# A chunked delta-rule attention on one core: the second chunk served by key and query products with the first chunk's keys in place of a state, and norm products of 96 columns

## The chip, the core and the metric

The kernel runs on one core of one Trainium2 chip, as one launch. The metric is the device time of that core in microseconds (us). The core has five engines with a queue each: TensorE (PE in the profile, with its weight loads as PEld), VectorE (DVE), ScalarE (ACT), GpSimd (POOL) and SyncE (SP), which issues the DMAs. All data are float32.

## What is computed

An input x of 4 sequences x 256 tokens x 256 channels goes through two layers. Each layer has a mixing part and an expert part, and each of the four parts sees its input scaled by a conditioning signal (a decaying two-way scan over the side input). The change lies in the mixing part of the first layer, a gated delta rule with 16 key heads and 32 value heads of 128 dimensions. The reference's scan over chunks, cut to its core:

```python
q = l2norm(q); k = l2norm(k)                  # norms over the 128 dimensions
A = where(strict, -(k_beta @ k.T) * decay, 0)  # within a chunk
attn = solve_triangular(eye - A, eye)
v_c, k_cumdecay = attn @ v_beta, attn @ (k_beta * exp(g))
def step(state, inp):
    attn_i = where(lower, q_i @ k_i.T * d_i, 0)
    v_new = v_i - kcd_i @ state
    o_i = q_i * exp(g_i) @ state + attn_i @ v_new
    state = state * exp(g_last) + (k_i * exp(g_last - g_i)).T @ v_new
    return state, o_i
```

The kernel uses chunks of 128 tokens, so a sequence has two: the first starts from a state of zero, and the only state that is ever read is the one after the first chunk. For the second chunk it holds that k_2 @ state and q_2 @ state are products of k_2 (or q_2) with k_1.T diag(decay) v_new_1.

## The kernel before, in words

The work is done in two halves, s = 0 and 1, of two sequences (b) each: 512 tokens. Attention is cut into units, one for each key head and half, so 32 units with two value heads (v) each; a tile of "four problems" holds v and b, 4 x 128 columns of 128 partitions. Four units make a Group, which does their 32x32 inverses together in one long chain of small VectorE operations (`small_inverses`). Then the units go two by two.

A unit (class Unit) goes through these functions:

- `products`: loads the key and query weights, makes the causal convolution of q and k (ps_cvq, ps_cvk, then ScalarE and three VectorE taps), and keeps both with their channels on partitions, one buffer kq for each chunk n (0 and 1), in which j is 0 for keys and 1 for queries. For each chunk, `gram` multiplies the keys with keys and queries of the same chunk (two products of 256 columns into ps_gram) and the copy `taken` puts them into kqm. `turn` transposes the first chunk's keys (two transposes) and sums the squares of keys and queries, a product with one column of ones for each of the 8 sums, all into ps_kt; a copy puts the transposed keys into k_tok. Then come the norms (k2, ki, kn, eo), the weights c and dc on POOL, and for each chunk the decay tile attnT, fetched by a broadcast DMA, exponentiated and multiplied with kqm on POOL. The products with keys go into the group's X, those with queries stay in attnT.
- `values`: v's convolution (ps_cvv), transposed into vo (ps_vt).
- `inverse` and `Group.inverse64`: 32x32 and 64x64 products (ps_lu, ps_lx, ps_lxu) that make X the full inverse.
- `outputs`: on POOL, kd is k_tok times the decay weight dc (`decayed`). TensorE makes the first new values vn0 = X vo (ps_vn), the state from kd and vn0 (ps_st, copied by ScalarE to state), the first chunk's output (ps_at), and the second chunk's keys with the state (ps_ks), which VectorE takes off the second chunk's values (`without`). Then vn1, and in `second` the second chunk's output from the queries (qe, which POOL multiplies with exp(g) in `queries`) with the state and from attnT with vn1. The gate product z (ps_z) is made here too.
- `normed`: squares summed on ScalarE, a root on POOL, four POOL products on vo, two transposes (ps_ot); `Group.project` multiplies with the output weights (ps_wo) and adds to x.

After attention class Rest does, for each half, 64 small experts, two to a product (ps_h, ps_a), a mixing layer (ps_in, ps_mix, ps_out) and 8 larger experts (ps_e, ps_ae), with routers (ps_lg, ps_w_wT).

The order of instructions on each engine is not the program's order. Every operation is recorded on a Tape with its engine, an estimated cost, the buffers that it reads and writes, a table of activation functions where it needs one, and for TensorE a density (`dense`, 0.12 for `turn`). `Tape.plan` lays all of them out by list scheduling with those costs, each engine taking the most urgent operation among those that could start first, with limits on how many buffers of a kind may be out at once (`MOST`, and PLACES for all tiles of 512 columns) and a penalty for thin TensorE work. Ten rounds are planned, the shortest plan is kept, and the instructions are issued in its order. Everything recorded there has line 128 in the profile, so the groups are told apart by the names of their tiles.

Of the kernel before, what the change touches and what calls it, by code (L numbers as in the profile page):

```python
# [181 lines left out]
class Tape:  # L182
# [11 lines left out]
    def op(self, engine, cost, emit, r=(), w=(), port=False, table=None, due=None, late=0.0, to=None, dense=1.0):  # L194
# [22 lines left out]
        if to is not None and to not in o.bufs:  # L217
            o.bufs.append(to)
            to.uses += 1
# [64 lines left out]
    def plan(self, latest):  # L284
# [17 lines left out]
        while todo:  # L302
# [4 lines left out]
            for e, ops in waiting.items():  # L307
# [10 lines left out]
                if best is not None and first >= best[0]:  # L318
                    continue
# [13 lines left out]
                if best is None or most[2] < best[0]:  # L333
                    best = (most[2], self.ops[most[1]])
# [5 lines left out]
            at, o = best  # L340
# [70 lines left out]
ROUNDS, SWITCH, LOAD, SPARE, AHEAD, EACH, END, IDLE, MOMENT, GAP, RATE, GIVES = 10, 14.0, 1.3, 90.0, 160.0, 15.0, 1300.0, 30.0, 0.8, 150.0, 4.0, 5.0  # L411
UNIT = 33.0
WINDOW, ENOUGH, LITTLE, SLOW, THIN = 3.4, 0.45, 0.38, 0.5, 10.0
# [261 lines left out]
class Unit:  # L675
# [83 lines left out]
    def products(self):  # L759
        p, s, h = self.p, self.s, self.h  # L760
        e, op = p.e, p.tape.op
        ident = p.const(IDENT)
# [14 lines left out]

        kqm = []
# [4 lines left out]
        for n in range(2):  # L783
            ps = p.ps(f"gram{n}_{self.tag}")
            m = self.buf([P, 2, 2, P], "kqm", 2, name=n)
            kqm.append(m)

            def gram(n=n, ps=ps):
                for b in range(2):
                    e.tensor.matmul(  # L790
                        ps()[:, b * 256 : b * 256 + 256],
                        kq[n]()[:, b, 0, :],
                        kq[n]()[:, b].rearrange("p j d -> p (j d)"),
                        start=True,
                        stop=True,
                    )

            op("PE", _mm(256, 2), gram, [kq[n]], [ps], to=m)

            def taken(m=m, ps=ps):  # L800
                copy(
                    m().rearrange("p j b d -> p b j d"),
                    ps().rearrange("p (b j d) -> p b j d", b=2, j=2),
                )

            op(*cost(512), taken, [ps], [m])

        self.k_tok = self.buf([P, 2, P], "k_tok", 5)
        ps = p.ps(f"kt_{self.tag}")
        sums = lambda j: ps()[:, 256 + 4 * j : 260 + 4 * j]  # L810
# [13 lines left out]
        def turn(ps=ps):  # L824
            for b in range(2):
                e.tensor.transpose(ps()[:, b * P : b * P + P], kq[0]()[:, b, 0, :], ident)
            for n in range(2):
                for j in range(2):
                    for b in range(2):
                        at = 2 * n + b  # L830
                        e.tensor.matmul(
                            sums(j)[:, at : at + 1],
                            sqs[n]()[:, b, j, :],
                            p.const(LT)[:, P - 1 :],
                            start=True,
                            stop=True,
                        )

        op("PE", 1.86, turn, [(kq[0], {0}), *sqs], [ps], to=self.k_tok, dense=0.12)
        op(  # L840
            *cost(256),
            lambda ps=ps: copy(
                self.k_tok(), ps()[:, :256].rearrange("p (b d) -> p b d", b=2)
            ),
            [ps],
            [self.k_tok],
        )
# [244 lines left out]
    def outputs(self):  # L1092
        p, s = self.p, self.s
        e, op = p.e, p.tape.op
        vo, kq, gate = self.vo, self.kq[1], p.gateb[s]
# [6 lines left out]
        def vob(n):  # L1102
            return vo[n]().rearrange("p v b d -> p (v b) d")
# [24 lines left out]
        kd = self.buf([P, 2, 2, P], "kd", 1)  # L1128

        def decayed():  # L1130
            w = self.dc().rearrange("p (v b) -> p v b", v=2).unsqueeze(3)
            e.gpsimd.tensor_tensor(
                kd(), _over(self.k_tok(), 1, 2), w.to_broadcast([P, 2, 2, P]), ALU.mult
            )

        op("POOL", 1.05, decayed, [self.k_tok, self.dc], [kd])
        vn0 = new_values(0, lambda: vob(0), vo[0])
        state = four("state", 1)
        ps = product(
            "st", lambda q: kd()[:, q // 2, q % 2, :], lambda q: vn0()[:, q, :], [kd, vn0], state  # L1140
        )
        copied(state, ps, state)
# [9 lines left out]
            lambda q: kq()[:, q % 2, 0, :],  # L1152
            lambda q: state()[:, q, :],
            [(kq, {0}), state],
# [31 lines left out]
        def queries():  # L1186
            to = qe().rearrange("p (v b) d -> p v b d", v=2)
            e.gpsimd.tensor_tensor(to, to, _over(kq()[:, :, 1, :], 1, 2), ALU.mult)

        op("POOL", 1.28, queries, [(kq, {1})], [qe])  # L1190
# [30 lines left out]
        def second():  # L1221
            for q in range(4):
                o = ps()[:, q * P : q * P + P]
                e.tensor.matmul(o, qe()[:, q, :], state()[:, q, :], start=True, stop=False)
                e.tensor.matmul(o, self.attnT[1]()[:, q, :], vn1()[:, q, :], start=False, stop=True)

        op("PE", 2 * cost, second, [qe, state, self.attnT[1], vn1], [ps])
# [80 lines left out]
class Program:  # L1308
# [85 lines left out]
    MOST = {"attnT": 20, "kq1": 10, "kq0": 4, "kqm": 8, "vo": 8, "zs": 6, "oT": 6, "w0": 6, "hw0": 8, "w1": 6, "hw1": 8}  # L1394
# [771 lines left out]
```

## Time and profile before

| what | value |
| --- | --- |
| median of 3 runs | 1534.3 us (1534.11, 1534.3, 1545.77) |
| the profiled execution's own time | 1536.94 us |
| its span in the profile | 1535.0 us |
| mean granted clock of TensorE | 0.957 |
| PE / DVE / ACT / POOL busy | 1431.9 / 1129.4 / 932.5 / 909.9 us |
| instructions | 24434 |
| ACT table loads | 106 at line 128, 136.0 us |

The span runs from the first to the last instruction of the profiled execution; 1.94 us of its time lie around it. An engine's busy time counts its instructions alone. The clock is the share of TensorE's full speed that was granted. A row of the groups gives the tile written and those read, the shape, the count, the busy time in us and the mean length of one in ns, then the idle time of the engine just before them and who ended it. Rows of TensorE show two records for each float32 product and one for a transpose, and their lengths overlap, so that the distance of two starts tells more than a length.

### The profile page before, as it was taken

The page shows a single profiled execution, that of the slowest core. Times are in us where ns is not written, and L with a number is a line of the kernel's source. Part 1 is how long each engine was busy: PE and PEld are TensorE (multiplying, and loading weights), DVE is VectorE, ACT ScalarE, POOL GpSimd, SP SyncE. Part 2 cuts the span into 40 slices and gives each one's busy share as a digit, 9 for nine tenths or more (in the row PEclk, how much of TensorE's full clock was granted, in tenths as well). Part 3 has the DMA queues.
Part 4 walks back from the last instruction along what each step waited for, and adds up shares of the span by engine and source line. Part 5 has one row for each costly group of instructions (what it writes and reads, how often), then busy time and mean ns, then how long its engine had stood idle before and what let it go on. Part 6 is the DMA issues. An engine that isn't in the chain of part 4 may idle for free.

```text
span 1535.0 us, 24434 instructions
## 1 busy us (share of the span) xinstructions
PE 1431.9 (93%) x8620; PEld 933.4 (61%) x8620; DVE 1129.4 (74%) x2117; ACT 932.5 (61%) x2037; POOL 909.9 (59%) x913
## 2 busy tenths in 40 slices
PE   4985999999999799999999999899999999999988
PEld 2643776876877577687777777686443443444433
DVE  7899889579578888988899868875777686343233
ACT  2685887888668788888888887886112441112120
POOL 3159778477483878869777568545766437133032
PEclk9987899999899999989999999899999999999999
DMA  6030212112030320312311222201564434691030
GB/s 211 9 118 7 67 59 83 43 54 64 12 114 15 98 83 25 100 58 68 94 46 57 82 76 84 79 13 36 147 171 137 130 107 130 168 276 50 0 110 14
DMA packets 79801, 126.52 MB, mean 82 GB/s; under 512 B 10032, under 2 KB 26160, under 8 KB 79680
## 3 DMA queue, kind: packets, MB, share of 16 engines
q1 hardware_dynamic: 78672, 123.81, 26.7%
q8 instruction: 68, 1.11, 0.3%
q10 hardware_dynamic: 1008, 1.16, 0.3%
q14 instruction: 53, 0.43, 0.1%
HBM read 120.31 MB, written 4.62 MB: 81 GB/s over the span
## 4 chain that ended last, share of the span: by engine, by line
PE 68%; DVE 17%; POOL 6%; ACT 5%; issue 2%; DMA 2%; SPq 1%; ACTq 0%; DVEq 0%; POOLq 0%
PE ps_wo L128 7%; PE ps_h L128 6%; PE ps_a L128 6%; PE ps_z L128 5%; PE ps_at L128 5%; PE ps_cvv L128 4%; PE ps_e L128 3%; PE ps_ae L128 3%; PE ps_vn L128 3%; PE ps_kt L128 3%; PE ps_cvq L128 2%; PE ps_gram L128 2%; POOL vo L128 2%; PE ps_cvk L128 2%; PE ps_in L128 2%
## 5 line engine op out<-in xcount | busy, mean ns | idle before, releaser
L128 DVE SCALAR_TENSOR_TENSOR accv_v<-ps_cvv,sb_convw,accv_v 128x510 f32<-128x510 f32 (+2 forms) x192 | 141.8, 741 | 16.8 <-ACT accv_v L128 11.7
L128 POOL TENSOR_TENSOR hw_h<-hw_h,r_h 128x512 f32<-128x512 f32 x64 | 84.2, 1318 | 111.8 <-DVE hw_h L128 110.4
L128 ACT ACTIVATE r_h<-ps_h 128x512 f32<-128x512 f32 x64 | 38.2, 597 | 183.7 <-PE ps_h L128 181.5
L128 ACT ACT_TABLE_LOAD x106 | 136.0, 1283 | 7.5 <-DVE sb_xT L128 3.6
L128 PE MATMUL ps_cvv<-ratio,wv 128*128 128x512 f32 x256 | 124.2, 614 | 2.3 <-issue 1.4
L128 PE MATMUL ps_z<-wz,ratio 128*128 128x256 f32 x512 | 119.6, 381 | 3.2 <-DVE accv_v L128 2.8
L128 PE MATMUL ps_h<-ratio,w_w 128*128 128x512 f32 x256 | 117.8, 600 | 3.1 <-DMA w_w<-in_w 3.0
L128 PE MATMUL ps_wo<-oT,wo 128*128 128x512 f32 x256 | 116.4, 608 | 0.0
L128 PE MATMUL ps_a<-hw_h,w_w 128*128 128x512 f32 x256 | 115.3, 593 | 0.7 <-POOL hw_h L128 0.7
L128 PEld LDWEIGHTS ps_z<-wz,ratio 128*128 128x128 f32 x512 | 94.7, 190 | 20.2 <-issue 4.5
L128 POOL TENSOR_TENSOR hw_e<-hw_e,r_e 128x512 f32<-128x512 f32 x32 | 40.5, 1279 | 86.8 <-DVE hw_e L128 86.8
L128 PEld LDWEIGHTS ps_h<-ratio,w_w 128*128 128x128 f32 x256 | 48.4, 192 | 64.3 <-issue 61.2
L128 PE MATMUL ps_gram<-kq 128*128 128x256 f32 x256 | 71.7, 420 | 16.9 <-ACT kqm L128 6.6
L128 DVE TENSOR_TENSOR xs<-xs,prod 128x30 f32<-128x30 f32 (+14 forms) x240 | 81.1, 338 | 8.2
L128 PEld LDWEIGHTS ps_a<-hw_h,w_w 128*128 128x128 f32 x256 | 48.5, 190 | 62.6 <-issue 56.2
L128 PE MATMUL ps_at<-vn,attnT 128*128 128x128 f32 x512 | 85.9, 282 | 0.1
L128 DVE SCALAR_TENSOR_TENSOR hw_h<-ps_h,wb_wb 128x512 f32<-128x512 f32 x64 | 43.7, 687 | 56.9 <-ACT r_h L128 50.8
L128 DVE TENSOR_TENSOR prod<-xs,Rt 128x30 f32<-128x30 f32 (+14 forms) x240 | 78.6, 328 | 9.1 <-ACT xs L128 2.8
L128 POOL TENSOR_TENSOR X<-attnT,kqm 128x512 f32<-128x512 f32 x64 | 84.1, 1333 | 1.9 <-PE ps_vn L128 1.6
L128 PEld LDWEIGHTS ps_wo<-oT,wo 128*128 128x128 f32 x256 | 49.5, 196 | 57.9 <-issue 52.8
L128 ACT ACTIVATE junko<-vo 128x128 f32<-128x128 f32 x256 | 79.3, 310 | 7.2
L128 POOL TENSOR_TENSOR vo<-vo,zs 128x512 f32<-128x512 f32 x64 | 82.3, 1306 | 0.0
(258 smaller groups left out, 3802.0 us busy)
## 6 DMA issues: line engine op xcount, KB each, us to landing
attnT<-G SPq DMA_DIRECT2D x64, 256.0 KB, 4.8
w_w<-in_w SPq DMA_DIRECT2D x64, 256.0 KB, 4.6
wb_wb<-w_rows SPq DMA_DIRECT2D x128, 128.0 KB, 4.1
wqk<-in_wqk SPq DMA_DIRECT2D x32, 256.0 KB, 3.5
wv<-in_wv SPq DMA_DIRECT2D x32, 256.0 KB, 3.0
wz<-in_wz SPq DMA_DIRECT2D x32, 256.0 KB, 2.8
wo<-in_wo SPq DMA_DIRECT2D x32, 256.0 KB, 3.1
qe<-G SPq DMA_DIRECT2D x32, 256.0 KB, 3.4
```

Source lines behind the costliest of these rows:

```text
L128: return self._tc.keep_in_program_order(f(*a, **k))
```

## The change

The state is not formed any more. In `products` a third gram is made for each unit, of the first chunk's keys with the second chunk's keys and queries (`cross`, copied like kqm, by VectorE for the first four units and by ScalarE for the rest); it shares an operation with the second chunk's own gram. The transposes of the first chunk's keys and the copy to k_tok go. In `outputs` the decay weight multiplies the first new values (vd, on POOL, which now reads vn0) in place of the keys, ps_ks is cross times vd, and qe takes the queries' part of cross in place of the queries, so that the second chunk's output is qe with vd. The product ps_st and its copy go.

The 8 sums of squares are now products with 96 columns of a triangle of ones, of which the last one is the sum; they are made from the last to the first, so that each leaves its sum in the column that later ones do not reach. The planner is told a density of 0.7 and a cost of 1.0 for them, where `turn` had 0.12 and 1.86.

The planner changes too: in its non-strict step it takes the engine whose best candidate is the most urgent instead of the one that starts first, an operation can hold several result buffers, and most of its constants and buffer limits have new values. With that the order of instructions is another one on every engine from the start on. Counted in the built programs, TensorE has 64 more products of 256 columns, 256 of 96 columns for 256 of one, 128 products of 128 columns and 64 transposes fewer; ScalarE has 32 copies of state and 28 of k_tok fewer, 28 of cross more, and 100 table loads where there were 108; VectorE has 4 copies of cross for 4 of k_tok; POOL has 32 vd for 32 kd; the DMAs are the same in number.

```diff
-ROUNDS, SWITCH, LOAD, SPARE, AHEAD, EACH, END, IDLE, MOMENT, GAP, RATE, GIVES = 10, 14.0, 1.3, 90.0, 160.0, 15.0, 1300.0, 30.0, 0.8, 150.0, 4.0, 5.0
-UNIT = 33.0
-WINDOW, ENOUGH, LITTLE, SLOW, THIN = 3.4, 0.45, 0.38, 0.5, 10.0
+ROUNDS, SWITCH, LOAD, SPARE, AHEAD, EACH, END, IDLE, MOMENT, GAP, RATE, GIVES = 10, 11.7, 1.3, 106.8, 160.0, 23.99, 1300.0, 30.0, 0.68, 150.0, 3.14, 5.0
+UNIT = 41.74
+WIDE = 96
+WINDOW, ENOUGH, LITTLE, SLOW, THIN = 3.4, 0.54, 0.38, 0.5, 10.0
...
-                if best is not None and first >= best[0]:
+                if self.strict and best is not None and first >= best[0]:
...
-                if best is None or most[2] < best[0]:
-                    best = (most[2], self.ops[most[1]])
+                first = most[2] if self.strict else latest[most[1]]
+                if best is None or first < best[0]:
+                    best = (first, most[2], self.ops[most[1]])
...
+        for pairs in (((0, 0),), ((1, 1), (0, 1))):
...
+                m = self.buf([P, 2, 2, P], "kqm" if n0 == n else "cross", 2, name=n0)
...
-            for b in range(2):
-                e.tensor.transpose(ps()[:, b * P : b * P + P], kq[0]()[:, b, 0, :], ident)
...
-                            sums(j)[:, at : at + 1],
-                            sqs[n]()[:, b, j, :],
-                            p.const(LT)[:, P - 1 :],
...
-        op("PE", 1.86, turn, [(kq[0], {0}), *sqs], [ps], to=self.k_tok, dense=0.12)
...
+            for at in reversed(range(8)):
+                j, n, b = at // 4, at // 2 % 2, at % 2
+                e.tensor.matmul(
+                    ps()[:, 505 + at - WIDE : 505 + at],
+                    sqs[n]()[:, b, j, :],
+                    p.const(LT)[:, P - WIDE :],
...
+        op("PE", 1.0, norms, sqs, [ps], dense=0.7)
...
-        op("POOL", 1.05, decayed, [self.k_tok, self.dc], [kd])
-        vn0 = new_values(0, lambda: vob(0), vo[0])
-        state = four("state", 1)
-        ps = product(
-            "st", lambda q: kd()[:, q // 2, q % 2, :], lambda q: vn0()[:, q, :], [kd, vn0], state
-        )
-        copied(state, ps, state)
+            e.gpsimd.tensor_tensor(vd(), vn0(), _over(self.dc(), 2, P), ALU.mult)
+        op("POOL", 1.06, decayed, [vn0, self.dc], [vd])
...
-            lambda q: kq()[:, q % 2, 0, :],
-            lambda q: state()[:, q, :],
+            lambda q: cross()[:, 0, q % 2, :],
+            lambda q: vd()[:, q, :],
...
-        op("POOL", 1.28, queries, [(kq, {1})], [qe])
+        op("POOL", 1.28, queries, [cross], [qe])
...
-                e.tensor.matmul(o, qe()[:, q, :], state()[:, q, :], start=True, stop=False)
+                e.tensor.matmul(o, qe()[:, q, :], vd()[:, q, :], start=True, stop=False)
...
-    MOST = {"attnT": 20, "kq1": 10, "kq0": 4, "kqm": 8, "vo": 8, "zs": 6, "oT": 6, "w0": 6, "hw0": 8, "w1": 6, "hw1": 8}
+    MOST = {'attnT': 20, 'kq1': 12, 'kq0': 2, 'kqm': 8, 'cross': 10, 'vo': 8, 'zs': 6, 'oT': 6, 'w0': 6, 'hw0': 8, 'w1': 6, 'hw1': 8, 'wo': 2, 'sq': 4, 'r0': 3, 'wqk': 20}
```

## The prediction

> **What bounds the kernel now.** I read the page's busy shares first, then the chain that ended last, then the windows by stage, then TensorE's groups and its timeline. From the page, PE's busy share and granted clock in 40 slices, and the chain by engine:
>
> ```profile
> PE 1431.9 (93%) x8620; PEld 933.4 (61%) x8620; DVE 1129.4 (74%) x2117; ACT 932.5 (61%) x2037; POOL 909.9 (59%) x913
> PEclk9987899999899999989999999899999999999999
> PE 68%; DVE 17%; POOL 6%; ACT 5%; issue 2%; DMA 2%; SPq 1%; ACTq 0%; DVEq 0%; POOLq 0%
> ```
>
> The windows by stage: from the first gates to the first new values, to 402, to the end of attention, the experts. After the length stand PE, PEld, DVE, ACT, POOL busy (with counts), PE's granted clock, DMA share and GB/s:
>
> ```profile
> 36.80:167.30 130.50, 103.25 (x593) 66.04 (x593) 115.02 (x233) 89.70 (x173) 76.53 (x78) 0.84 0.15 48
> 167.30:402.00 234.70, 230.68 (x1873) 174.91 (x1873) 188.07 (x359) 199.69 (x461) 166.82 (x168) 0.99 0.19 56
> 402.00:1068.00 666.00, 646.16 (x5077) 488.10 (x5076) 551.21 (x1071) 526.91 (x1212) 457.13 (x464) 0.96 0.21 65
> 1068.00:1535.00 467.00, 437.46 (x1035) 194.71 (x1033) 247.34 (x412) 105.43 (x177) 195.78 (x186) 0.97 0.41 119
> ```
>
> From 167 us on TensorE is busy 96% of the time and no other engine over 85%: a microsecond of TensorE work, or of its clock, is a microsecond of time. Only from 36.8 to 167 is VectorE the bound (115 of 130.5 us busy); there TensorE work is nearly free. The clock has places of its own; in windows of PE alone, the third number is its busy time, the one after the count its clock:
>
> ```profile
> 402.00:420.00 18.00, 17.89 (x185) 0.62 0.02 4
> 552.00:558.00 6.00, 6.00 (x71) 0.72 0.11 37
> 666.00:684.00 18.00, 18.00 (x268) 0.72 0.24 75
> 792.00:804.00 12.00, 12.00 (x156) 0.72 0.30 86
> ```
>
> PE is busy in these and yet granted 0.62 to 0.72. In each the timeline shows a run of thin products just before: 32x32 and 64x64 tiles of the inverses, and in the last three a ps_kt, whose products have one column. The loss is 18 x 0.38 + 6 x 0.28 + 18 x 0.28 + 12 x 0.28 = 16.9 us.
>
> Prices, from the timeline at full clock (start, length, operation; the step to the next start is the price):
>
> ```profile
> 258.54 0.44 PE L128 MATMUL ps_kt<-sb_consts,kq 128*128 128x128 f32 x2 [0.34 <-ACT oT L128]
> 258.82 1.84 PE L128 MATMUL ps_kt<-sb_consts,sq 128*128 128x1 f32 x16
> 260.52 7.11 PE L128 MATMUL ps_wo<-oT,wo 128*128 128x512 f32 x16
> 267.47 3.62 PE L128 MATMUL ps_gram<-kq 128*128 128x256 f32 x16
> 271.02 0.69 PE L128 MATMUL ps_lu<-Tc,X 32*32 32x32 f32 x32
> 273.47 1.04 PE L128 MATMUL ps_vt<-sb_consts,accv_v 128*128 128x128 f32 x8
> 274.35 1.89 PE L128 MATMUL ps_z<-wz,ratio 128*128 128x256 f32 x8
> ```
>
> A matmul has two records. 16 one-column records step 1.70 us (0.106 each); 8 of 128 columns 0.88 (0.110 each); 16 of 256 columns, which are four gram operations, 3.55 (0.89 each; 0.865 at 221.33, which I take).
>
> **The change, part by part.** 32 units run it.
>
> *TensorE work.* Gone per unit: two transposes of k_tok (0.21 at 175.83) and the four products st (8 records, 0.90 at 230.97). Added: the cross gram, 0.865. 32 x (0.865 - 1.11) = -7.8 us. The norms keep 16 records; with 96 columns a record lies between 0.106 and 0.110, so 0 to +0.07 a unit, 0 to +2 us; I take 0, since 96 columns are less than the 128 that already hide.
> By the Trainium skill's page "TensorE: Matmul & The Clock Gate", section "Back-to-back issue gap", a product costs N / 2.4 + 2.5 ns with a floor of 25 ns; one column would then cost 25 and 96 columns 42.5 ns, which as an estimate is 16 x 17.5 ns x 32 = 9 us more, and the time 1512. The rows do not agree with it (106 ns for one column); the Trainium skill's section "LDWEIGHTS (loading the stationary operand)" on that page, with 128 columns / 1.2 = 107 ns, agrees with them.
>
> *ScalarE, VectorE, POOL, DMA.* The copies of state (32 x 0.578) and k_tok (28 x 0.369) go, 28 copies of cross (0.583 like kqm) come: ACT -12.5 us, and 8 fewer table loads in the built order, -10.3. VectorE gets 4 cross for 4 k_tok, +1.1. POOL gets vd for kd, both 512 elements, 1.05. DMAs and SP's order length are unchanged. All of it lies beside TensorE, which hides it: ACT has 35 us of 235 free even in its fullest stage. If TensorE ran out, the order of waits would decide, as below.
>
> *The moved wait.* Before: vn0 copied, st, state copied, then ks. Now: vn0 copied (0.58), vd on POOL (1.05), then ks: with 0.17 drain and handoffs of 0.02 to 0.07 some 2.0 us. POOL is in order, so behind a vd that waits for vn0 stand the next units' attnT and X; ks, and after it VectorE's subtraction and vn1, wait for vd. In the built order the TensorE work between vn0 and ks, at the prices above, is 2.6 to 2.7 us in ten units, 3.4 us in seven, more in the others (before: 3.5 the least, mostly over 5). Slack is 0.6 in the ten. If the POOL operation ahead (1.3 us) is just starting, a tight unit waits 0.7. Bounds 0 and (10 x 0.7 + 7 x 0.6) = 11 us; the trace of before has ks waiting 0.5 us in all, so nearer the low end: +4.
>
> *The start.* The planner's new constants move everything. Up to the first 32x32 product (lu of unit 0), TensorE now has 81 us of work in front where it had 72 (the cross grams of eight units, one more norm, one more convolution), all in the stage that VectorE bounds. VectorE's rows up to Tc sum to 3.8 us more (4 cross for k_tok, and ratio pieces drawn ahead). Ends: -9.3 and +3.8; I take -9.3 + 3.8 = -5.5.
>
> *The clock.* In the built order I listed each 3.4 us of TensorE's work that is mostly thin, from the first inverse on. With one-column norms counted thin, before has long runs at four places, which are the four windows above, one for one. After has two runs, both without norms: lx, lu, lu64, lx of units 12 and 13 in the first half, and lx, lu, lxu64 of the same units in the second, 3 to 4 us each. Price of each between 0 and the 6.8 of the worst; nearest is the short run at 552, 1.7. So -16.9 + 3.4 = -13.5, ends -16.9 and -3.3.
> Around 668 the clock in windows of 1.7 us reads 0.96, five times 0.50, 0.52, 1.00. The Trainium skill's page "TensorE: Matmul & The Clock Gate", section "What's actually happening", has the clock either half or full, set by free-running windows of 3.4 us; these rows agree on the two values, and no row here shows the window, which would leave runs of 3 to 4 us to chance.
>
> *The experts.* The last pair of units now stands among the first half's later layers. Gone: the wait for POOL before the last ot at 1068 to 1086 (4.4 idle + 3.4 clock), and the two gaps before in and lg at 1194 to 1206 and 1236 to 1254 (6.1 + 5.1): -19.0. New: the second half's first router stands bare. Its logits wait as the last ones do at 1458 to 1470 (1.8 + 1.4), and its ranking, about 12 us of ACT and DVE rows, has only hs and two h (4 x 1.72) beside it: 5.1 idle and some 2.6 of clock. +10.9, net -8. Ends -19 (hidden) and +11 (nothing gone).
>
> Sum: -7.8 - 5.5 - 13.5 - 8 + 4 = -30.8. The profiled execution's span of 1535.0 becomes 1504.2, its own time 1506.1 (1.94 around the span); the median shown is 2.6 lower than that execution, so 1503.5.
>
> **Rivals.**
> A. The clock is not won: the gate counts something that 96 columns do not feed, or new thin places appear. For: the first of the four windows has no norm. Against: three have one. Time 1503.5 + 13.5 = 1517.
> B. The other side: POOL becomes the wait. If a vd stands behind three POOL operations that its own unit could not foresee (X and both attnT, 3.9 us), ks can start 5.9 after vn0 where it has 2.6 us of work in ten units, 3.4 in seven, 4.4 in six: 10 x 3.3 + 7 x 2.5 + 6 x 1.5 = 60 us, 56 more than counted: 1560. It decides at 31 / 32, about 1 us a unit on the average. For: 2.6 us is little room, and POOL's vo stands in the chain for 4 to 5 us at 423, 584 and 707. Against: POOL is busy only 69 to 71% of these stages, and of TensorE's idle time up to 1068 hardly 4 us (before ps_ot) are put down to it.
> C. The new order brings new stalls like those at 498 to 516 (4.7 idle, 3.4 clock) in five or so places, or the bare router costs 20 more: about 1530.
> D. The wide norms do not do what they say but cost by column: 256 against 128 columns is 0.825 ns a column, so 95 x 0.825 x 16 x 32 = 40 us on top: 1543. Against: the 128-column record at 0.110. The Trainium skill's issue-gap rule named above is a milder form of this, at 1512.
> E. More is won: starts and gaps at their good ends (-9.3, -16.9, -19, 0): 1482.
>
> **Numbers.** Forecast 0.58 (own range 1488 to 1518), A 0.14, B 0.07, C 0.11, D 0.03, E 0.07. Predicted 1503.5. The range 1482 to 1532 leaves out B, D and halves of C and of E, 0.19. One per cent is about what a measurement of this kernel can tell from no change. Faster, under 1519: 0.54 of the forecast, 0.09 of A (1517 with its own spread), E: 0.70. Within 1%, to 1549.6: the rest of A and of the forecast, D, most of C: 0.20. Slower: B and 0.03 of C where its stalls are long: 0.10.
>
> **What would show it.** Right: ps_kt with 16 records still 1.70 apart; no ps_st; granted clock over 0.98 between 402 and 1000; PE's work from lu of unit 0 to the end some 17 us less. Wrong: ps_ks with idle time before it released by POOL vd (B); clock near 0.5 after norms (A); ps_w_wT or ps_lg of the second half with over 10 us idle (C); ps_kt over 1.8 (D).

## The result and the profile after

| | before | changed |
| --- | --- | --- |
| median (range) | 1537.95 us of 4 runs (1534.11 to 1545.77) | 1490.91 us of 4 runs (1489.44 to 1493.29) |
| ratio of the times, 95% interval | | 0.9689 (0.9643 to 0.9736) |
| profiled execution: its time, its span | 1536.94, 1535.0 | 1490.23, 1488.1 |
| mean granted clock of the profiled execution | 0.957 | 0.974 |
| table loads of ScalarE at line 128 | 106, 136.0 us | 98, 125.7 us |

The changed kernel is 3.1% faster. The forecast was 1503.5 with a range of 1482 to 1532, so the time fell 12.6 us under the forecast and inside the range. The gain was half as large again as forecast: 47 us by the medians, where 30.8 had been added up. The experiments ask what brought it.

From the page of the changed kernel, the same three lines as before:

```profile
PE 1401.1 (94%) x8428; PEld 901.6 (61%) x8428; DVE 1122.8 (75%) x2117; ACT 911.2 (61%) x1997; POOL 915.1 (61%) x913
PEclk9997899999999899999999999999999999999999
PE 76%; DVE 15%; DMA 3%; issue 2%; ACT 2%; POOL 1%; SPq 0%; DVEq 0%; POOLq 0%; ACTq 0%
```

TensorE has 192 matmul records fewer and a larger share of the chain (76% where it was 68%); POOL's share of the chain fell from 6 to 1%, though POOL now multiplies the new values between two TensorE products of every unit. In the row of the clock only one slice after the start, near 500 us, stands below 9.

The windows by stage of the changed kernel, the first one again up to the first new values (length, then PE, PEld, DVE, ACT, POOL busy, the clock, DMA share, GB/s):

```profile
36.80:170.50 133.70, 115.07 (x598) 76.97 (x599) 118.30 (x239) 94.36 (x180) 80.19 (x81) 0.83 0.17 53
170.50:402.00 231.50, 230.41 (x1853) 174.21 (x1851) 186.90 (x363) 193.28 (x455) 171.29 (x172) 1.00 0.20 59
402.00:1068.00 666.00, 649.67 (x4749) 455.86 (x4748) 556.15 (x1066) 493.12 (x1134) 468.48 (x466) 0.99 0.27 81
1068.00:1488.00 420.00, 391.57 (x1185) 184.50 (x1183) 233.53 (x409) 119.73 (x212) 181.56 (x178) 0.98 0.35 105
```

Between 402 and 1068 the clock is 0.99 where it was 0.96, and the stage after it is granted 0.98. The stages are cut at fixed times, so in another order they do not hold quite the same work: the last ps_vn of attention starts at 1175.9 here, and at 1063.3 before. The same four places as before, and the one new loss, in windows of TensorE alone (busy time is the second number, the clock the one after the count):

```profile
402.00:420.00 18.00, 18.00 (x217) 1.00 0.33 102
498.00:516.00 18.00, 13.18 (x173) 0.72 0.00 1
552.00:558.00 6.00, 6.00 (x52) 1.00 0.01 1
666.00:684.00 18.00, 18.00 (x121) 1.00 0.12 38
792.00:804.00 12.00, 12.00 (x48) 1.00 0.15 45
```

Four of the five read 1.00. The window at 498 holds the thin run that the prediction had named for the first half (lx, lu, lu64, lx, from 505.11 to 511.82). But the clock was low before that run began:

```profile
500.83 1.06 PE L128 MATMUL ps_vt<-sb_consts,accv_v 128*128 128x128 f32 x8 [2.45 <-DVE vo L128]
501.73 1.75 PE L128 MATMUL ps_gram<-kq 128*128 128x256 f32 x4
503.27 1.91 PE L128 MATMUL ps_gram<-kq,kq 128*128 128x256 f32 x4
```

From 503.27 a gram takes 1.84 us to the next start, where it takes 0.865 at full clock. What stands ahead of it is one operation of 32x32 products (at 497.69) between waits of 1.09 and 2.45 us. So this loss followed waits more than thin products.

Rows of TensorE's groups of the changed kernel (busy us, mean ns, then idle time before them and who ended it):

```profile
L128 PE MATMUL ps_kt<-sb_consts,sq 128*128 128x96 f32 x512 | 65.8, 284 | 5.2 <-ACT sq L128 4.5 <-ACT oT L128 0.3 <-ACT kqm L128 0.2
L128 PE MATMUL ps_ks<-vd,cross 128*128 128x128 f32 x256 | 34.2, 277 | 0.4 <-DVE accq_q L128 0.4
L128 PE MATMUL ps_lg<-sb_gateT,ratio 128*128 128x64 f32 x32 | 4.4, 281 | 2.3 <-DVE ratio L128 2.0 <-DVE vo L128 0.3
L128 PE MATMUL ps_w_wT<-sb_consts,wb_route 128*64 128x128 f32 x8 | 1.7, 347 | 7.3 <-DVE wb_route L128 7.3
```

ps_ks waited 0.4 us in all, and not for vd. The router without other TensorE work beside it, which the prediction expected, is there: ps_w_wT waits 7.3 us and the logits 2.3.

To see where the 46.9 us of span went, I cut TensorE's time after 36 us into windows of 6 us. In each, idle is what it was not busy, clock is busy time x (1 - granted clock), and the rest of the span is work at full clock:

| us | before | changed | difference | forecast |
| --- | --- | --- | --- | --- |
| 36 to 174: idle / clock | 28.0 / 16.9 | 19.4 / 18.3 | -7.2 | start -5.5 |
| 174 to 402: idle / clock | 4.0 / 0.0 | 1.1 / 0.0 | -2.9 | |
| 402 to 1068: idle | 19.8 | 16.4 | -3.4 | ks +4 |
| 402 to 1068: clock | 25.7 | 4.2 | -21.5 | clock -13.5 |
| 1068 to the end: idle / clock | 29.5 / 11.3 | 28.4 / 6.4 | -6.0 | experts -8 |
| work at full clock | 1363.8 | 1357.9 | -5.9 | work -7.8 |

By this table over half of the gain is TensorE's clock (25.0 us of 46.9), and no term has the wrong sign except that of ks. A table of two traces does not show what caused a term, though, and a row varies from one execution to the next: in five executions of the changed kernel's order (this one, e1, e5, e6, e12) the clock up to 174 us lost 11.0 to 18.3 us.

### The profile page after: what moved, and what is told of

The parts are those of the page before. It is cut to its first block, busy times and chain, and to the rows that moved or that the text cites. A ratio compares the mean times of both kernels' runs of the same rounds, so it can differ in the third digit from the quotient of the medians.

```text
span 1488.1 us, 23985 instructions
## 1 busy us (share of the span) xinstructions
PE 1401.1 (94%) x8428; PEld 901.6 (61%) x8428; DVE 1122.8 (75%) x2117; ACT 911.2 (61%) x1997; POOL 915.1 (61%) x913
## 4 chain that ended last, share of the span: by engine, by line
PE 76%; DVE 15%; DMA 3%; issue 2%; ACT 2%; POOL 1%; SPq 0%; DVEq 0%; POOLq 0%; ACTq 0%
PE ps_cvv L128 6%; PE ps_wo L128 6%; PE ps_z L128 6%; PE ps_h L128 6%; PE ps_at L128 5%; PE ps_gram L128 5%; PE ps_a L128 4%; PE ps_ae L128 4%; PE ps_cvq L128 4%; PE ps_kt L128 4%; PE ps_cvk L128 4%; PE ps_vn L128 3%; PE ps_e L128 3%; PE ps_lu L128 2%; PE ps_lx L128 2%
## 5 line engine op out<-in xcount | busy, mean ns | idle before, releaser
L128 ACT ACT_TABLE_LOAD x98 | 125.7, 1283 | 16.6 <-DVE sb_xT L128 7.0
L128 PE MATMUL ps_z<-wz,ratio 128*128 128x256 f32 x512 | 123.1, 386 | 1.0 <-ACT zs L128 0.8
L128 PE MATMUL ps_wo<-oT,wo 128*128 128x512 f32 x256 | 113.4, 594 | 0.0
L128 PEld LDWEIGHTS ps_z<-wz,ratio 128*128 128x128 f32 x512 | 93.0, 190 | 14.8 <-issue 1.5
L128 POOL TENSOR_TENSOR vd<-vn,dc 128x512 f32<-128x512 f32 x32 | 33.9, 1060 | 92.3 <-ACT vn L128 92.3
L128 POOL TENSOR_TENSOR attnT<-attnT,kqm 128x512 f32<-128x512 f32 x64 | 82.4, 1300 | 0.9
L128 PE MATMUL ps_at<-vn,attnT 128*128 128x128 f32 x512 | 81.4, 276 | 0.0
```

What stands on the lines that cost most here:

```text
L128: return self._tc.keep_in_program_order(f(*a, **k))
```

## The experiments

Theory 1 is that of the prediction: the parts of the change each bring a term of their own (less TensorE work, wide norms that hold the clock, an order with better start and experts). Theory 2: the wide norms do nothing, the order alone spread the thin products. Theory 3: the planner's constants and rule brought nearly all of it, by an order that fits this algebra. Ratios are to the kernel before, with 95% intervals.

### Norms of one column in the changed order (e1)

```diff
-WIDE = 96
+WIDE = 1
```

> The changed kernel with its norms back to products of one column (WIDE = 1), the planner's figures and so the order of every engine as in the changed kernel. Theory 1 (the wide columns hold the clock): three places of the second half where a norm stands with 32x32 and 64x64 products (near 576, 700 and 818 us) fall back to a granted clock of 0.6 to 0.8, some 2 to 6 us each, and up to three shorter ones; less 32 x 0.05 us for the shorter steps of a norm: 6 to 14 us slower than the changed kernel, 1497 to 1505, ratio to the kernel before 0.973 to 0.978. Theory 2 (the order alone spread the thin products): within 2 us of the changed kernel, the clock between 402 and 1068 at 0.99.

Measured 1497.85 us (1496.63 to 1500.57 in 6 runs), ratio 0.9744 (0.9721 to 0.9768): 7 us slower than the changed kernel by the medians, 8.5 by the ratios, as theory 1 has it. The timeline of e1 around the first loss shows how:

```profile
472.19 1.84 PE L128 MATMUL ps_kt<-sb_consts,sq 128*128 128x1 f32 x16
474.76 1.06 PE L128 MATMUL ps_ot<-sb_consts,vo 128*128 128x128 f32 x8 [0.73 <-DVE k L128]
476.17 2.69 PE L128 MATMUL ps_kt<-sb_consts,sq 128*128 128x1 f32 x16 [0.34 <-ACT oT L128]
478.72 3.76 PE L128 MATMUL ps_wo<-oT,wo 128*128 128x512 f32 x4
```

Two norms with 0.9 us of other work and two short waits between them; from the second one on the products take twice as long (four records of ps_wo in 3.76 us). The same instructions of the changed kernel:

```profile
470.14 1.92 PE L128 MATMUL ps_kt<-sb_consts,sq 128*128 128x96 f32 x16
472.73 1.07 PE L128 MATMUL ps_ot<-sb_consts,vo 128*128 128x128 f32 x8 [0.67 <-DVE k L128]
474.14 2.02 PE L128 MATMUL ps_kt<-sb_consts,sq 128*128 128x96 f32 x16 [0.34 <-ACT oT L128]
476.00 7.06 PE L128 MATMUL ps_wo<-oT,wo 128*128 128x512 f32 x16
```

The waits are the same and the clock stays (16 records of ps_wo in 7.06 us). In e1 this place and one more, where two norms stand with one gram between them, lose clock:

```profile
474.00:486.00 12.00, 10.93 (x36) 0.72 0.00 1
528.00:540.00 12.00, 12.00 (x80) 0.86 0.43 105
```

Two later runs, e5 and e6, keep the order and the 96 columns, and both places read 1.00 in them as in the changed kernel: three executions with wide norms lost nothing there. The three places that I had named first, near 576, 700 and 818, lost nothing: the clock there reads 1.00. The size of the effect was as expected, the places were not.

### Norms of 96 columns in the order before (e2)

```diff
-                            sums(j)[:, at : at + 1],
-                            p.const(LT)[:, P - 1 :],
+                    ps()[:, 409 + at : 505 + at],
+                    p.const(LT)[:, P - 96 :],
```

> The kernel before with its norms made 96 columns wide and nothing else; the planner's figures and the order as before. Theory 1 (wide columns hold the clock): the three windows with a norm, 552 to 558, 666 to 684 and 792 to 804, which lose 10.1 us in the kernel before, keep most of it; the first, 402 to 420, has no norm and stays near 0.62; norms cost 32 x 0.05 = 1.6 us more: 5 to 9 us faster, 1526 to 1530. Theory 2 (order alone): same to 2 us slower, the three windows unchanged. If a record cost by column: 40 us slower.

Measured 1530.48 us (1524.71 to 1541.5 in 12 runs), ratio 0.9965 (0.9941 to 0.9989): 5.4 us faster by the ratios, at the low end of theory 1, against theory 2. But the windows tell more than either theory said. Of the profiled execution of e2 (one 4 us faster than its median):

```profile
402.00:420.00 18.00, 17.23 (x215) 1.00 0.11 32
552.00:558.00 6.00, 6.00 (x59) 1.00 0.65 221
666.00:684.00 18.00, 17.73 (x195) 1.00 0.46 154
774.00:792.00 18.00, 14.77 (x151) 0.72 0.14 39
```

The first window reads 1.00 too, and it has no norm; the last one before it lies some 28 us earlier in both kernels. The products that lead into it are the same in both kernels, in the same order with the same waits of about 1 us. Before:

```profile
398.72 0.95 PE L128 MATMUL ps_lx<-X,U 32*32 32x32 f32 x32
400.63 1.16 PE L128 MATMUL ps_vn<-vo,X 128*128 128x128 f32 x8 [0.97 <-ACT X L128]
401.72 1.64 PE L128 MATMUL ps_lx<-X,T 64*64 64x64 f32 x16
403.48 2.08 PE L128 MATMUL ps_at<-vn,attnT 128*128 128x128 f32 x8
```

and in e2:

```profile
397.73 0.94 PE L128 MATMUL ps_lx<-X,U 32*32 32x32 f32 x32
399.64 1.16 PE L128 MATMUL ps_vn<-vo,X 128*128 128x128 f32 x8 [0.97 <-ACT X L128]
400.73 1.14 PE L128 MATMUL ps_lx<-X,T 64*64 64x64 f32 x16
402.48 1.16 PE L128 MATMUL ps_at<-vn,attnT 128*128 128x128 f32 x8 [0.61 <-ACT vn L128]
```

In the one the clock falls within the 64x64 products and ps_at steps twice as slowly, in the other it stays. So the same thin run can bring a loss or none, and nothing in these traces tells which. e2 also has a new loss at 774, behind a wait of 3.4 us for VectorE. And clock that is won is not all time: between 402 and 1068 e2 loses 15.4 us less by the clock than the kernel before and stands idle 10.4 us longer. The mean clock of whole executions shows the wide norms' part with less of that chance: 0.956 over the 17 executions of the kernel before beside e1 to e4 (0.951 to 0.964, and the longer ones have the lower clock: correlation -0.88), 0.964 over the 12 of e2; 0.968 over the 6 of e1, 0.975 over the 4 of the changed kernel. The wide norms are worth 0.007 to 0.008 of clock in these two orders.

### How wide (e12)

```diff
-WIDE = 96
+WIDE = 32
```

> The changed kernel with norms of 32 columns in place of 96, order unchanged. If the clock follows the share of columns in use (a quarter here), the two places where e1 lost it, two norms with a short operation between them at 474 to 486 and 528 to 540, fall again to about 0.7 to 0.86: 1495 to 1499, ratio 0.972 to 0.975. If it takes only a product with more than one column: 1489 to 1493, clock there 1.00, ratio 0.968 to 0.971. A norm's 16 records step 1.70 to 1.75 us either way.

Measured 1495.23 us (1493.64 to 1497.42), ratio 0.9732 (0.9704 to 0.976): the first outcome, though only one of the two places fell (0.72 at 474 to 486, 1.00 at 528 to 540). The mean clocks for 1, 32 and 96 columns are 0.968, 0.971 and 0.975. A norm's 16 records step 1.70, 1.70 and 1.75 us (the norm near 255 us in each). So the extra columns cost 0.05 us a unit, 1.6 us in all. By the clocks, what they buy grows with their number; by the ratios, 32 columns and one cannot be told apart (0.9732 and 0.9744, with intervals that overlap).

### The new algebra in an order made by the old planner (e3)

```diff
-ROUNDS, SWITCH, LOAD, SPARE, AHEAD, EACH, END, IDLE, MOMENT, GAP, RATE, GIVES = 10, 11.7, 1.3, 106.8, 160.0, 23.99, 1300.0, 30.0, 0.68, 150.0, 3.14, 5.0
-UNIT = 41.74
+ROUNDS, SWITCH, LOAD, SPARE, AHEAD, EACH, END, IDLE, MOMENT, GAP, RATE, GIVES = 10, 14.0, 1.3, 90.0, 160.0, 15.0, 1300.0, 30.0, 0.8, 150.0, 4.0, 5.0
+UNIT = 33.0
...
-                if self.strict and best is not None and first >= best[0]:
+                if best is not None and first >= best[0]:
```

ENOUGH, the second part of the rule, and MOST (with 10 for cross) go back as well.

> The changed kernel's algebra and its norms of 96 columns, with the planner's rule, constants and limits of the kernel before (limit 10 for cross). Theory 1 (each part brings its own term): work -7.8, clock between 402 and 1068 some -15, no gain at the start or in the experts, whose order is again the one of the kernel before: 1510 to 1518, ratio about 0.985. Theory 3 (the new constants and rule brought nearly all of it, the algebra only its work): 1524 to 1530, ratio above 0.99. A third outcome, ks late behind vd in the order that was not made for it: above 1534.

Measured 1554.53 us (1553.33 to 1558.3), ratio 1.0117 (1.0091 to 1.0142): 18 us slower than before, where theory 1 had expected some 20 faster. The third outcome is the nearest in time, but not for its reason: ps_ks waited 0.0 us. Rows of e3:

```profile
L128 PE MATMUL ps_kt<-sb_consts,sq 128*128 128x96 f32 x512 | 65.6, 284 | 26.1 <-ACT sq L128 22.8 <-ACT kqm L128 2.9 <-ACT oT L128 0.3
L128 PE MATMUL ps_in<-ratio,w_win 128*128 128x512 f32 x64 | 30.0, 621 | 14.9 <-DVE ratio L128 14.8
L128 PE MATMUL ps_lg<-sb_router,ratio 128*128 128x8 f32 x32 | 6.7, 339 | 14.1 <-DVE ratio L128 14.0
```

One norm of the start waits 22.6 of the 26.1 us. ScalarE's timeline shows what stands ahead of the squares (sq) that it needs:

```profile
114.94 0.63 ACT L128 ACTIVATE attnT<-attnT 128x512 f32<-128x512 f32 x1 [1.24 <-DVE attnT L128]
...
124.63 0.63 ACT L128 ACTIVATE attnT<-attnT 128x512 f32<-128x512 f32 x1 [3.01 <-DVE attnT L128]
...
131.35 0.63 ACT L128 ACTIVATE sq<-kq 128x512 f32<-128x512 f32 x1
...
134.20 0.63 ACT L128 ACTIVATE sq<-kq 128x512 f32<-128x512 f32 x1 [1.61 <-POOL attnT L128]
```

The decay tiles attnT go first, and most of them wait for VectorE. The first 32x32 product comes at 177.5 us where it came at 149.7 before. In the experts ps_in and ps_lg wait 14.8 and 14.0 us for ratio, their input as the conditioning scales it. Between 402 and 1068, idle and clock lose 28.7 us where they lost 45.5 before: the middle gains, as theory 1 says, and what lies before and after it gives back more (26.1 us between 174 and 402 and 21.2 us from 1068 on).

### The old algebra in an order made by the new planner (e4)

The kernel before with the constants, the rule and the limits of the changed one (the reverse of the diff above, without cross).

> The kernel before (state, transposed keys, norms of one column), with the planner's rule, constants and limits of the changed kernel. Theory 1: only start (-5.5), experts (-8) and what the order alone does to the clock: 1515 to 1527, with drops of the clock where norms meet small products. Theory 3 (constants and rule brought nearly all of it): 1497 to 1505.

Measured 1552.03 us (1548.51 to 1558.8), ratio 1.0094 (1.0066 to 1.0122): slower than before, against theory 1 and theory 3 both. Between 402 and 1068 it loses 31.3 us idle and 21.8 of clock (before 19.8 and 25.7), in a dozen places; the worst window, with a one-column norm among waits, holds 7.6 us of that clock:

```profile
768.00:786.00 18.00, 15.99 (x74) 0.53 0.07 15
```

So algebra and wide norms with the old planner cost 18 us, the new planner with the old algebra costs 14, the wide norms alone bring 5, and all together bring 48. The terms do not add. That constants and algebra have to fit is the reading that is left, and the next runs ask how much of the gain is this fit.

### One constant nudged (e7)

```diff
-ROUNDS, SWITCH, LOAD, SPARE, AHEAD, EACH, END, IDLE, MOMENT, GAP, RATE, GIVES = 10, 11.7, 1.3, 106.8, 160.0, 23.99, 1300.0, 30.0, 0.68, 150.0, 3.14, 5.0
+ROUNDS, SWITCH, LOAD, SPARE, AHEAD, EACH, END, IDLE, MOMENT, GAP, RATE, GIVES = 10, 11.7, 1.3, 106.8, 160.0, 23.99, 1300.0, 30.0, 0.70, 150.0, 3.14, 5.0
```

> The changed kernel with one planner constant nudged: MOMENT 0.70 in place of 0.68, which gives another order of all engines and the same work. Theory 3 (the gain hangs on a fit of the constants to this algebra, and orders near it are worse): 10 to 30 us slower than the changed kernel, 1501 to 1521. Theory 1 (any order of this kind would have the gain): within 5 us of 1491.

Measured 1507.78 us (1506.23 to 1509.84), ratio 0.9803 (0.9781 to 0.9826): 17 us slower than the changed kernel, with the same work, from 0.02 in one constant. By the table's measure it has 12.3 us more idle time, 7.8 of them between 402 and 1068 (24.2 where it was 16.4). That is theory 3's outcome.

### The old algebra with constants of its own (e8)

```diff
-ROUNDS, SWITCH, LOAD, SPARE, AHEAD, EACH, END, IDLE, MOMENT, GAP, RATE, GIVES = 10, 14.0, 1.3, 90.0, 160.0, 15.0, 1300.0, 30.0, 0.8, 150.0, 4.0, 5.0
-UNIT = 33.0
+ROUNDS, SWITCH, LOAD, SPARE, AHEAD, EACH, END, IDLE, MOMENT, GAP, RATE, GIVES = 10, 13.186, 1.3, 86.034, 160.0, 15.0, 1300.0, 30.0, 0.801, 150.0, 4.262, 5.222
+UNIT = 39.868
...
-                if best is not None and first >= best[0]:
+                if self.strict and best is not None and first >= best[0]:
```

ENOUGH becomes 0.385, THIN 9.579, and oT, w1, hw1, wo, sq, r0, wqk are limited to 8, 8, 9, 4, 6, 3, 7. They were chosen for a short plan by the planner's own costs, with norms of one column, state and transposed keys.

> The algebra of the kernel before (state, transposed keys, norms of one column) with the changed selection rule and with constants and limits that fit it better than either set so far. Theory 1 (algebra and wide columns bring their own terms of 8 us each, and the rest is order): 1503 to 1515, ratio 0.977 to 0.985. Theory 3 (order is all): 1488 to 1500. If neither rule nor constants matter by themselves: 1530 to 1545.

Measured 1503.62 us (1499.8 to 1505.33), ratio 0.9772 (0.9747 to 0.9797). Nothing of the new algebra and no wide norm is in it, and it has 2.3 of the changed kernel's 3.1%. It falls in theory 1's interval and misses theory 3's, so order is not shown to be all. But about three quarters of the gain can be had by order alone.

### The same with wide norms (e9)

The edit of e2 on e8.

> The retuned version of the old algebra (e8) with its norms 96 columns wide and nothing else, so the same order. Theory 1 (wide columns hold the clock wherever two norms stand close, in either algebra): clock losses of e8 behind norms go, 3 to 8 us faster than e8, 1496 to 1501, ratio to the kernel before 0.972 to 0.975. Theory 2: within 2 us of e8. What is then left to the changed kernel is the worth of the algebra alone: 5 to 10 us by the work and the price of added TensorE work that e6 showed (18.9 us for 27.7).

Measured 1504.36 us (1503.95 to 1506.9), ratio 0.9794 (0.9767 to 0.9821), the mean clock of its executions 0.968 against 0.970 of e8: nothing gained. Theory 2's outcome. Between 402 and 1068 e8 loses 8.9 us of clock and e9 7.9, at the same three places (504 to 522, 528 to 546 and 642 to 660). TensorE waits at each of them (in e8 it is 1.8 us busy of 6 at 504, 4.7 at 528 and 3.4 at 648), and in e8 the last norm ends over 10 us ahead of each. So wide norms had little to win in this order; in e1's order, with two norms close together, they had.

### Is POOL's new operation near the path (e5)

```diff
             e.gpsimd.tensor_tensor(vd(), vn0(), _over(self.dc(), 2, P), ALU.mult)
+            e.gpsimd.tensor_tensor(vd(), vn0(), _over(self.dc(), 2, P), ALU.mult)
```

> The changed kernel with the multiplication that makes vd issued twice on POOL (same result), so that vd is ready 1.04 us later in every unit; order unchanged. Theory 1 (ks stands with room behind vd): from the trace of the changed kernel, 10 of 32 units have under 1.04 us between the end of vd and the start of ks, and what they lack sums to 4 us; with knock-on on VectorE 3 to 8 us slower than the changed kernel, 1494 to 1499, ratio to the kernel before 0.972 to 0.975. Rival B (POOL is nearly the wait): 25 to 35 us slower, 1516 to 1526, with idle time before ps_ks released by POOL vd.

Measured 1502.16 us (1498.29 to 1504.64), ratio 0.9764 (0.9738 to 0.9789): 11 us slower than the changed kernel for 32 x 1.12 us more on POOL. Two groups of e5:

```profile
L128 PE MATMUL ps_ks<-vd,cross 128*128 128x128 f32 x256 | 36.3, 286 | 6.4 <-POOL vd L128 6.3
L128 PE MATMUL ps_lu<-Tc,X 32*32 32x32 f32 x1024 | 22.8, 195 | 10.5 <-DVE Tc L128 8.0 <-DVE X L128 1.4 <-DVE acck_k L128 1.1
```

Rival B is refuted: a vd of twice the length makes ks wait 6.3 us in all. Theory 1's 4 us for ks were near, but the time is 3 us above its interval. Of the 10.8 us of idle time that e5 has more than the changed kernel, 6.6 stand up to 174 us (ps_lu waits 8.0 us for Tc where it waited 5.0), but the clock lost 7.3 us less there. So it is not quite settled where the 11 us lie. In the changed kernel vd starts 0.07 to 0.08 us after the copy of vn0 in 23 of 32 units, and in 18 units it ends 0.7 to 1.7 us before ks starts: the order had left the room.

### Is a microsecond of TensorE work a microsecond (e6)

```diff
                 for n0, n, ps, _ in of:
                     gram(n0, n, ps)
+                    if n0 != n:
+                        gram(n0, n, ps)
```

> The changed kernel with the cross gram computed twice (the second one writes the same sums over the first), which adds 0.865 us of TensorE work to each unit; order unchanged. Theory 1 (a microsecond of TensorE work is a microsecond of time behind the start stage): the first eight units' cross grams lie in the start stage and cost little, the other 24 cost 0.865 each: 20 to 28 us slower than the changed kernel, 1511 to 1519, ratio 0.983 to 0.988. Rival (TensorE's waits take much of it up, so that the work term of the sum is worth nothing): under 10 us slower.

Measured 1507.56 us (1505.65 to 1509.05), ratio 0.9797 (0.9771 to 0.9823): 16.6 us by the ratios and 18.9 by the profiled spans, for 27.7 us of added work. It missed theory 1's interval by 1 to 3 us. Idle time fell by 5.0 us (65.3 to 60.3): TensorE's waits took a part of the added work up. So a microsecond of it cost 0.6 to 0.7 us of time over all 32 units; if the first eight cost nothing, as the expectation had it, one behind the start cost 0.8 to 0.9. By that the work term of the forecast is worth an estimated 5 to 7 us in place of 7.8.

### Better orders for the new algebra (e10, e11)

e10 gives the experts' part other limits and two other constants:

> The changed kernel with GAP 83.3, THIN 9.8 and the limits of w0, hw0, hw1 and r0 moved (8, 13, 6, 4): attention keeps its order nearly, the experts' part gets another. If the tail has room of its own: 4 to 9 us faster than the changed kernel, 1482 to 1487, with less idle time between 1068 and the end (28.4 us there in the changed kernel). If near orders are worse, as with e7: 1495 to 1510.

Measured 1487.52 us (1487.24 to 1490.1), ratio 0.9685 (0.9648 to 0.9721), the same as the changed kernel within the intervals. From 1068 on idle time fell only by 2.1 us (28.4 to 26.3), where the expectation wanted 4 to 9.

e11 tells the planner the measured price of a norm and takes constants that go with it:

```diff
-        op("PE", 1.0, norms, sqs, [ps], dense=0.7)
+        op("PE", 1.75, norms, sqs, [ps], dense=0.9)
...
-ROUNDS, SWITCH, LOAD, SPARE, AHEAD, EACH, END, IDLE, MOMENT, GAP, RATE, GIVES = 10, 11.7, 1.3, 106.8, 160.0, 23.99, 1300.0, 30.0, 0.68, 150.0, 3.14, 5.0
-UNIT = 41.74
+ROUNDS, SWITCH, LOAD, SPARE, AHEAD, EACH, END, IDLE, MOMENT, GAP, RATE, GIVES = 10, 13.03, 1.3, 106.8, 151.066, 23.307, 1300.0, 37.71, 0.688, 150.0, 3.14, 3.959
+UNIT = 40.014
```

ENOUGH is 0.513, and attnT, kq1, kqm, zs, w0, w1, hw1, sq, wqk are limited to 21, 11, 6, 7, 12, 10, 10, 2, 21.

> The changed algebra with the planner told the norm's measured step (1.75 us in place of 1.0, density 0.9) and constants that fit that. In its order the second half's router has some 44 us of other TensorE work between its logits and its turn, where the changed kernel has almost none. Theory 1: the router's 12 us of idle time and clock go, the rest stays: 1474 to 1482, ratio 0.958 to 0.963. Theory 3 (the changed kernel's order was already the fit): 1486 to 1500.

Measured 1475.98 us (1475.12 to 1480.33), ratio 0.9611 (0.9579 to 0.9642): faster than both kernels, 15 us under the changed one by the medians and 12 by the ratios. Its router has work beside it:

```profile
L128 PE MATMUL ps_lg<-sb_gateT,ratio 128*128 128x64 f32 x32 | 3.8, 272 | 0.0
L128 PE MATMUL ps_w_wT<-sb_consts,wb_route 128*64 128x128 f32 x8 | 1.2, 276 | 0.0
```

From 1068 on idle and clock lose 22.4 us where the changed kernel lost 34.8, which is the 12 us expected, and 402 to 1068 loses 14.6 where it lost 20.6; the stage before 402 gives back 10.8. That sums to -7.6; the other 7.0 us of the span stand in the work at full clock (1350.9 against 1357.9), which is the same work. That column is not better than some 5 us (e5 and e7, with the TensorE work of the changed kernel, read 1362.6 and 1361.8), so these 7 us are not explained. The told price and density, eight constants and nine limits changed at once, so e11 does not show which of them made the better order.

## Why the prediction was right, and where not

The time came inside the range because the prediction had read the built order: the work ahead of the first inverse, the thin places that were gone, the router without cover. Its terms had the right sign, all but that of ks. The span fell by 46.9 us where 30.8 were forecast; of the 16.1 us between, 8.0 are the clock, 7.4 the idle time from 402 to 1068 (ks), 4.6 the start up to 402, and the work and the experts take back 1.9 and 2.0. Point by point:

- **TensorE work, -7.8.** The rows moved as worked out (no ps_st, one gram more), except that a norm's step went from 1.70 to 1.75 us: +1.6, within the 0 to +2 that the prediction had allowed. That makes -6.2, and the table reads -5.9, in a column that is good to some 5 us. From the first lu to the end the work is some 15 us less, where 17 were named as a sign. Rival D, a cost by column, is out. What failed is the price, "a microsecond of TensorE work, or of its clock, is a microsecond of time": e6 shows 0.6 to 0.7 us for one of work, and in e2 two thirds of the clock won between 402 and 1068 turned into idle time.
- **Start, -5.5.** First lu at 154.1 where it was 149.7, 4.4 us later (3.8 forecast). Idle time up to 174 us fell by 8.6, near the 9.3 of the forecast's low end; idle time and clock together fell by 7.2 there, and by 2.9 more up to 402. The step was right and the size about half of what came.
- **Clock, -13.5.** Mis-sized: 21.5 us in the stage from 402 to 1068. The four windows went as forecast, 16.9. Three smaller losses of the kernel before that the sum had left out went too: 1.6 at 426 to 438, 3.0 at 504 to 516 and 4.2 at 984 to 996. For the two thin runs that were left the forecast had put 3.4; 4.2 came, all of it at 498 to 516, and there the clock fell behind waits before the thin run began, so that this number is near by luck. Nor does the step "four windows above, one for one" hold as a rule: e2 shows the first of them at 1.00 with the same products. And the 21.5 us are not all the wide norms': e1 and e2 price those at 5 to 8.5 us, the rest came with the order. Rival A asked whether the gate feels 96 columns; it does, by the mean clocks of e1, e12 and the changed kernel and by the two places of e1.
- **Experts, -8.** Measured -6.0. The router without cover cost 7.3 us before its turn, 2.3 before the logits and, between 1254 and 1272, 2.3 of clock: 11.9 against 10.9. What went was less than 19.0: by the table's measure the three places lost 17.7, since the prediction took the low clock over whole windows and so counted their idle part in both.
- **ks, +4.** Nothing was lost there. The bounds were made for a POOL operation standing ahead of vd, and vd started at once in 23 units.
- **The sum itself.** It took the terms of one order and called them the change's parts. e3 and e4 refute that reading: with the old planner the new algebra is 18 us slower than the kernel before, and the old algebra with the new planner 14. The forecast could be right since it was made on the built order and not on the algebra; e7 shows that an order next to it would have cost 17 us more.

What stays open: how much of the 3.1% the algebra is worth. From the best order found for the old algebra (e8, norms of one column, 0.9772) to the changed kernel (0.9689) it is about 0.8%, and to the best order found for the new one (e11, 0.9611) 1.6%. But more sets of constants were weighed for the new algebra than for the old, and one nudged constant (e7) moved the time by as much as 1.1%, so neither is a price of the algebra. The many small losses of e4 were not taken apart.

## What to carry to other kernels

When a change comes with new constants of a planner, price the order that was built, not the edit, and expect that the edit alone or the constants alone can lose. Split them on the chip before crediting either: here each alone was about 1% slower, together 3% faster, and the old algebra with constants of its own had 2.3%. And tell the planner measured prices where there are some: with the norm told at the 1.75 us that it takes, in place of 1.0, and constants to go with it, an order was found that is 15 us better, though which of the two found it was not tried.

## What the runs showed of the hardware

- TensorE's clock can fall while TensorE is busy all the time: in the kernel before from 666 to 684 (18.00 us busy of 18, clock 0.72), in e1 from 528 to 540 (12.00 of 12, clock 0.86), where two norms of one column stand close together.
- The same products with the same waits once kept the clock and once lost it (402 to 420: 0.62 before, 1.00 in e2). 17 executions of the kernel before spread from 1526.96 to 1542.16 us with clocks of 0.964 to 0.951. The Trainium skill's page "TensorE: Matmul & The Clock Gate", section "What's actually happening", calls the window of the gate free-running, and lets the point where the clock rises depend on where in it the first product lands. Such a spread would fit that, but no run here shows the window. For the fall that section speaks of idle windows; at the two places above TensorE was not idle.
- A product of one column and one of 96 take nearly the same time (16 records in 1.70 and 1.75 us), yet the wider ones held the clock better (mean 0.968 and 0.975, 32 columns between them at 0.971).
- At the low clock the records of a norm step twice as slowly too: in e12 the 16 records of the norm at 475.50 took 3.43 us to the next product where the others take 1.70.
